# Four-layer convolution network on one core: one of every four hidden-layer evictions of the last stage moved from ScalarE to VectorE

## The chip, the cores and the metric

The kernel runs on one core of a Trainium2 chip, in one launch. Its time is the device time of that core in microseconds (us). Several executions are timed, and the median counts; one further execution is recorded by the hardware profiler, and all durations below come from that one.

## What is computed

The input is a batch of 1024 images of 16 x 16 positions with 16 channels, in float32. Four layers follow each other, each of the form x + layer(group norm of x). Layer 0 is a tensor-train product, layer 2 a 3 x 3 convolution, and layers 1 and 3 are one step of a cellular automaton. Layer 3 is the one that the change touches:

```python
def update(x):
    xt = jnp.transpose(x, (0, 3, 2, 1))
    B, _, W, Hh = xt.shape
    pre = _alive(xt)                       # 3x3 maximum of channel 3 > 0.1
    y1 = _depthwise(xt, conv1_w, conv1_b)
    y2 = _depthwise(xt, conv2_w, conv2_b)
    p = jnp.concatenate([xt, y1, y2], axis=1)
    flat = p.reshape(B * W * Hh, 48)
    h = jax.nn.relu(flat @ fc0_w.T + fc0_b)          # 128 hidden values
    d = (h @ fc1_w.T + fc1_b).reshape(B, C, W, Hh)
    xn = xt + d
    mask = (pre & _alive(d)).astype(xn.dtype)
    return jnp.transpose(xn * mask, (0, 3, 2, 1))
...
x = x + _L3_conv_ref(_gn(x), ...)
```

The reshape to 48 columns is taken as it stands: a "pixel" of the hidden layer is three neighbouring rows of the flattened array, so a hidden row r (there are 256) depends on rows 3r, 3r+1 and 3r+2 of the channels and their two depthwise results.

## The kernel before, in words

The batch is worked on in two chunks of 512 images, one image per column of a tile of 128 x 512. The stages follow each other on TensorE without a break; normalization, loads and stores of neighbouring chunks are woven in. The last stage is layer 3 on the second chunk (`layer_nca(X1, 1, 3, L3, xo)`, L1729). It alone is called with `xo`, the buffer in which the result is turned for the output. It takes 2735.4 to 3003 us of the profiled span.

**Quads.** The 256 hidden rows are grouped in fours, the quads (q, w2, v, hf): q counts four groups of channels, w2 eight pairs of columns, v the two of a pair. Quad m holds the rows j = 0 to 3 of `rows_of` (L1343); "row m.j" below is row j of quad m. Quads 0 to 15 are q = 0, 16 to 31 q = 1, and so on. In this stage the last four quads are cut in halves of 256 images (hf = 0 or 1), so there are 68 quads, of which 0 to 59 have full width (hf is None).

**Hidden rows (fc0, L1562).** A row needs two or three matmuls (L1562, `ph`), each of 32 input rows, so four rows run side by side in four row groups of the array (32 input rows each). In q = 0 most rows have two, later three. The row is summed in a PSUM bank of pool `h`, six banks. After the last matmul it is evicted: relu of the sum plus bias, into a `hid` tile (128 x 512, pool of eight). This is L1565, on ScalarE (`A.activation`).

**Second matrix (fc1, L1398).** For each quad four matmuls side by side read its four `hid` tiles into a bank of pool `o` (two banks), which is shared by the two quads v = 0 and v = 1 of one column pair. After v = 1, `finish` (L1404) reads the bank on VectorE: in q = 0 the alive flags of the result (L1406), always the sum with the layer's input (L1410).

**Masks (q = 0 only).** For each column pair the flags of the input (L1428, VectorE) and of the result are counted over neighbours by small matmuls (`pcnt`, L1437) into two banks of pool `h`, and VectorE makes the mask from the two counts (L1442, L1443). Then GpSimd applies it and adds the residual (L1449, L1450); in q > 0 it does so directly after L1410.

**Turning.** Each finished tile is transposed on TensorE (`ptx`, L1460, into a bank of pool `o`), and VectorE copies it out in two halves (L159; in this stage the helper `evac` uses VectorE alone). Beside that, `output_steps` turns the first chunk: for each of 16 image lines SP loads a tile, VectorE transposes it in four instructions (L1041), and SP stores it (L1046).

**Order.** Every engine works through its own queue in the order in which the program issues the instructions (`manual_schedule`). For this stage the order comes from `plan()` (L1489). It yields one step at a time: either the fc1 of a quad, or a list of at most four tiles, one for each row group. It knows the six banks and a model of the evictions: an eviction begins at the earliest 1.15 steps after the row's last tile, evictions follow each other at 0.75 steps, and a bank is free at the end of its eviction. Rows up to two quads ahead of the next fc1 may begin:

```python
evacs = max(evacs, t + (1.15 if quads[m][3] is None else 1.9))
evacs += 0.75 if quads[m][3] is None else 1.0
free_at.append(evacs)
```

The plan orders TensorE's matmuls, and with them the evictions: `tile_of_row` (L1539) issues an eviction directly after the last matmul of its row. Calls put off with `after(n, ...)` are issued n steps later, after that step's own work: the mask three steps after an fc1, the turning eight steps after the residual. `run` (L1575) issues the steps of `output_steps` at fixed shares of the stage's 262 steps: the transposes of line n after a share of 0.068 + 0.054 n.

Two rules of the pools are needed to follow the prediction. A bank or tile that is freed goes to the back of its pool's line, and the next use takes the one at the front; which use frees or takes first is a matter of program order. If all eight `hid` tiles are still held in program order, the eviction takes the one that was taken longest ago, and waits for the fc1 that reads it, though TensorE comes to that fc1 only later.

Of the kernel before, what the change touches and what calls it, by code (L numbers as in the profile page):

```python
# [11 lines left out]
AF = mybir.ActivationFunctionType  # L12
ALU = mybir.AluOpType
# [46 lines left out]
def row_tiles(r):  # L60

    lines = defaultdict(list)
    for s in range(3):
        ch, w = divmod(3 * r + s, S)
        if ch < C:
            lines[ch, w].append(s)
        else:
            for kw in range(3):
                if 0 <= w + kw - 1 < S:
                    lines[ch, w + kw - 1].append((s, kw))  # L70
    tiles = defaultdict(lambda: [None, None])
    for (ch, w), terms in lines.items():
        what = terms[0] if ch < C else TERMS.index(tuple(sorted(terms)))
        tiles[ch, w // 2][w % 2] = what
    return [(ch, pair, tuple(v)) for (ch, pair), v in sorted(tiles.items())]
# [13 lines left out]
def triple(wo):  # L89

    k, w = divmod(3 * wo, S)
    if w >= S - 2:
        n = 2 if w == S - 1 else 3
        return n, 12 + 3 * n
    return w % 2, 6 * k + 3 * (w % 2)
# [8 lines left out]
def conv_preact_kernel(ctx: ExitStack, tc: tile.TileContext, a: dict, out: bass.AP):  # L104
    nc = tc.nc
    V, A, G, T = nc.vector, nc.scalar, nc.gpsimd, nc.tensor
# [29 lines left out]
    def work(shape, tag, name, dt=F32):  # L136
        p, sizes = pool["sb"]
        return p.tile(shape, dt, tag=tag, name=name, bufs=sizes[tag])
# [3 lines left out]
    def bank(shape, tag, name):  # L142
        p, sizes = pool["ps"]
        if tag == "mw":
            either[0] ^= 1
            tag = "mw"[either[0]]
        return p.tile(shape, F32, tag=tag, name=name, bufs=sizes[tag])
# [61 lines left out]
    for d, v in ((0, 1), (2, 0)):  # L209
# [7 lines left out]
    nca = dict(  # L217
        xw=pack[:, 0:512].rearrange("p (n k) -> p n k", n=4),
        b1=pack[:, 512:513],
        bt=pack[:, 513:769],  # L220
        w1=pack[:, 769:833].rearrange("p (v m) -> p v m", v=2),
    )
# [1102 lines left out]
    def layer_nca(X, n, l, L, xo=None):  # L1325
# [9 lines left out]
        def cols(hf):  # L1335
            return slice(0, NB) if hf is None else slice(hf * NB // 2, (hf + 1) * NB // 2)

        def width(hf):
            return slice(0, NB if hf is None else NB // 2)
# [3 lines left out]
        def rows_of(q, w2, v):  # L1343
            return [16 * (4 * q + j) + 2 * w2 + v for j in range(4)]

        def weights(m):

            if m >= len(quads):
                return
            q, w2, v, hf = quads[m]  # L1350
            slot = triple(2 * w2 + v)[1]
            if hf == 1:
                st["wq", m] = st["wq", m - 4]
            elif q > 0:
                st["wq", m] = work([P, 3, HID], "wq", "wq")
                nc.sync.dma_start(
                    st["wq", m],
                    L["wy"][q - 1].rearrange("g v h s k -> (g v h) s k")[:, slot : slot + 3],
                )

        def lines(m):


            if m >= len(quads) or triple(2 * quads[m][1] + quads[m][2])[0] < 2:
                return
            nx = st["nx", m] = work([P, 2, NB], "nx", "nx")
            for r in rows_of(*quads[m][:3]):
                tiles = row_tiles(r)
                g = tiles[0][0] % 4
                over = [t[0] % C for t in tiles if t[0] % 4 != g]  # L1370
                c, n1 = over[0], len(over)
                nc.sync.dma_start(
                    nx[32 * g : 32 * g + 32, 0:n1],
                    X[32 * (c % 4) : 32 * (c % 4) + 32, 8 * (c // 4) : 8 * (c // 4) + n1],
                )
# [50 lines left out]
        def flags(w2):  # L1426
            f = st["f", w2] = work([P, NB], "f", "flags", BF16)
            V.tensor_scalar(f[96:128], X[96:128, w2], ALIVE, None, ALU.is_gt)  # L1428
# [92 lines left out]
        def step(slot):  # L1521
            def go():
                t = st["slot"]
                if isinstance(slot, int):
                    q, w2, v, hf = quads[slot]
                    fc1(q, w2, v, hf, [st["hid", slot, j] for j in range(4)])
                else:
                    for x in slot:
                        tile_of_row(*x)
                go.dense = isinstance(slot, int)  # L1530
                due = [fn for n, fn in later if n <= t]
                later[:] = [x for x in later if x[0] > t]
                for fn in due:
                    fn()
                st["slot"] = t + 1

            return go

        def tile_of_row(m, j, k):  # L1539
            q, w2, v, hf = quads[m]  # L1540
            r = rows_of(q, w2, v)[j]
            tiles = row_tiles(r)
            if k == 0:
                if st.setdefault("begun", -1) < m:
                    st["begun"] = m
                    weights(m + AHEAD)
                    lines(m + FAR)
                    if v == 0 and q == 0:
                        flags(w2)
                st["ph", m, j] = bank([P, NB], "h", "ph")[:, width(hf)]  # L1550
            ph = st["ph", m, j]
            ch, pair, pat = tiles[k]
            g = tiles[0][0] % 4
            rg = slice(32 * g, 32 * g + 32)
            if ch < C:
                w = nca["xw"][rg, XPATS.index(pat)]
            else:
                w = st["wq", m][rg, TRIPLES[triple(2 * w2 + v)[0]].index(pat)]

            x = X[rg, 8 * (ch % C // 4) + pair] if ch % 4 == g else st["nx", m][rg, pair]  # L1560
            x = x[:, cols(hf)]
            T.matmul(ph, w, x, start=k == 0, stop=k == len(tiles) - 1)  # L1562
            if k == len(tiles) - 1:
                h = st["hid", m, j] = work([P, NB], "hid", "hid")[:, width(hf)]
                A.activation(h, ph, AF.Relu, bias=nca["bt"][:, r : r + 1])  # L1565

        def rest():
            while later:
# [156 lines left out]
    with ExitStack() as es:  # L1725
        stage(es, dict(nca_sb, xs=2, xo=2), nca_ps)

        xo = X0.rearrange("p n b -> p (n b)").rearrange("p (g h w c) -> p g h w c", g=4, h=S, w=S)
# [29 lines left out]
```

## Time and profile before

| what | us |
|---|---|
| median of 3 runs | 3019.41 |
| lowest and highest run | 3018.77, 3025.02 |
| profiled execution | 3020.7 |
| its span, first to last instruction | 3018.9 |
| mean granted TensorE clock, share of full speed | 0.991 |
| last stage, in the span | 2735.4 to 3003 |
| TensorE busy there | 264.4 of 267.6 |
| ScalarE busy there | 166.9 |
| VectorE busy there | 118.0 |
| 240 full-width evictions on ScalarE there, L1565 | 153.5, 0.686 each |
| 32 half-width evictions there | 13.5, 0.472 each |

The page of a profile gives for each engine its busy time, the share of the span and the number of instructions; below that the span in 40 equal slices, where a digit is the busy share of a slice in tenths; then the chain of work that ended last, followed back from the last instruction. A group line has the source line, engine, operation, output and inputs, shapes and count, then the busy time in us and the mean of one in ns, then the idle time just ahead of these instructions with what ended it. A line of the timeline has the start in us, the duration in us, and in square brackets the idle time before it with its releaser. PE is TensorE's matmul, PEld its weight load, DVE VectorE, ACT ScalarE, POOL GpSimd. In the table by stretch the columns are the stretch, its length, and the busy time of PE, PEld, DVE, ACT and POOL with the number of instructions, then the granted clock, the share of DMA and GB/s. Ends of matmuls are modelled, so a TensorE that is shown busy can still be waiting; starts are not modelled. A float32 matmul has two records.

### The profile page before, as it was taken

The numbers are of one execution on the slowest core, as the hardware profiler recorded it, in microseconds if no ns is written. First come the engines' busy times: TensorE is split into PE (matmuls) and PEld (weight loads), VectorE is DVE, ScalarE is ACT, GpSimd is POOL, SyncE is SP. The second block draws the span as 40 slices with busy tenths as digits, with TensorE's granted clock in tenths as the row PEclk, the third lists the DMA queues.
The fourth block names the chain that finished last, engine by engine and source line by source line (L and its number), as shares of the span: only waits on it lengthen the run. The fifth ranks groups of instructions, "written<-read, shape, count | busy, mean of one in ns | idle before, by whom it ended". The sixth has DMA issues, their size and how long they took to land.

```text
span 3018.9 us, 36939 instructions
## 1 busy us (share of the span) xinstructions
PE 2968.3 (98%) x13876; PEld 1247.0 (41%) x13876; DVE 1765.1 (58%) x2352; ACT 1102.6 (37%) x1822; POOL 669.5 (22%) x727
## 2 busy tenths in 40 slices
PE   7999999999999999999999999999999999999997
PEld 5544334444444444444444433333333333333333
DVE  5354337555554555544555768856878766856433
ACT  4431441000000000000111146666667666666564
POOL 2035670200000000000000005434542323442321
PEclk8999999999999999999999999999999999999998
DMA  8643664533334433332222234445446866443466
GB/s 317 232 127 94 152 150 146 167 110 110 110 110 138 138 110 110 110 103 89 89 89 94 72 124 161 129 133 194 131 131 177 196 100 211 129 129 110 135 173 215
DMA packets 251523, 418.40 MB, mean 139 GB/s; under 512 B 34869, under 2 KB 105065, under 8 KB 248273
## 3 DMA queue, kind: packets, MB, share of 16 engines
q1 hardware_dynamic: 225776, 362.53, 36.6%
q0 software_dynamic: 25376, 53.38, 8.6%
q8 instruction: 110, 1.80, 0.3%
q14 instruction: 69, 0.56, 0.1%
q10 hardware_dynamic: 192, 0.13, 0.0%
HBM read 238.58 MB, written 165.53 MB: 134 GB/s over the span
## 4 chain that ended last, share of the span: by engine, by line
PE 90%; issue 2%; DVE 2%; DMA 2%; POOL 1%; ACT 1%; SPq 0%; POOLq 0%; DVEq 0%; ACTq 0%
PE po L1172 51%; PE ph L1562 21%; PE po L1398 8%; PE po L1260 3%; PE pw L1095 3%; PE L_conv_pe L392 1%; PE ptin L902 1%; PE po L1269 1%; DMA xn<-xf 1%; PE ptx L1460 1%; POOL res L1450 1%; POOL u L1449 1%; DVE sq L622 1%; PE pr L801 0%; DMA xn<-in_x_dram 0%
## 5 line engine op out<-in xcount | busy, mean ns | idle before, releaser
L1172 PE MATMUL po<-xn,w 128*128 128x512 f32 x3584 | 1577.4, 597 | 0.8 <-DVE xn L982 0.8
L1172 PEld LDWEIGHTS po<-xn,w 128*128 128x128 f32 x3584 | 671.7, 190 | 839.5 <-issue 820.9
L1565 ACT ACTIVATE hid<-ph,pack 128x512 f32<-128x512 f32 (+1 forms) x1040 | 655.6, 680 | 375.1 <-PE ph L1562 263.7
L1208 DVE TENSOR_TENSOR r<-r,po 128x512 f32<-128x512 f32 x576 | 378.2, 684 | 577.1 <-PE po L1172 524.7
L1449 POOL TENSOR_TENSOR u<-u,mask 128x512 f32<-128x512 f32 x123 | 193.8, 1576 | 1809.1 <-DVE mask L1443 1410.9
L1100 ACT COPY w<-pw 128x512 f32<-128x512 f32 (+1 forms) x320 | 150.6, 557 | 1209.6 <-issue 1006.4
L1562 PE MATMUL ph<-xn,wq 32*128 32x512 f32 (+1 forms) x3752 | 565.2, 599 | 0.0
L1562 PEld LDWEIGHTS ph<-xn,wq 32*128 32x128 f32 x3752 | 240.7, 184 | 263.9 <-issue 231.8
L1562 PE MATMUL ph<-xn,pack 32*128 32x512 f32 x1288 | 299.2, 625 | 4.6 <-DVE mask L1442 3.2
L1398 PE MATMUL po<-hid,pack 128*32 128x512 f32 (+1 forms) x2080 | 279.4, 600 | 0.0
L1113 DVE TENSOR_TENSOR w<-w 128x512 f32<-128x512 f32 x320 | 211.3, 687 | 86.6 <-ACT w L1100 86.6
L655 DVE TENSOR_TENSOR xn<-xn,m 128x1024 f32<-128x1024 f32 x160 | 216.3, 1383 | 35.5 <-ACT m L678 35.3
L1450 POOL TENSOR_TENSOR res<-res,u 128x512 f32<-128x512 f32 x123 | 204.5, 1663 | 9.6
L1410 DVE SCALAR_TENSOR_TENSOR u<-po,pack,xn 128x512 f32<-128x512 f32 (+1 forms) x130 | 96.3, 741 | 179.2 <-PE po L1398 175.1
L1260 PE MATMUL po<-xn,convw 128*128 128x512 f32 x368 | 163.9, 598 | 2.7 <-ACT conv L1310 2.7
L1562 PEld LDWEIGHTS ph<-xn,pack 32*128 32x128 f32 x1288 | 115.6, 186 | 105.2 <-issue 67.4
L1208 DVE TENSOR_TENSOR xn<-xn,po 128x512 f32<-128x512 f32 x96 | 64.4, 685 | 123.7 <-PE po L1172 123.3
L1398 PEld LDWEIGHTS po<-hid,pack 128*32 128x32 f32 x2080 | 42.8, 108 | 192.2 <-issue 134.3
L622 DVE TENSOR_TENSOR sq<-sq 128x1024 f32<-128x1024 f32 x75 | 106.2, 1416 | 11.1 <-ACT sq L640 10.4
L1260 PEld LDWEIGHTS po<-xn,convw 128*128 128x128 f32 x368 | 68.2, 190 | 97.8 <-issue 88.1
L404 POOL DMA_DIRECT2D L_conv_wy<-xn x160 | 88.8, 563 | 28.3 <-ACT xn L398 17.0
L1095 PE MATMUL pw<-R,gq 32*128 32x256 f32 (+1 forms) x1280 | 89.1, 384 | 1.0 <-DMA gq<-g_dram 1.0
(174 smaller groups left out, 1776.7 us busy)
## 6 DMA issues: line engine op xcount, KB each, us to landing
xf<-r SPq DMA_DIRECT2D x112, 512.0 KB, 3.8
xn<-xf SPq DMA_DIRECT2D x96, 512.0 KB, 4.7
r<-xf SPq DMA_DIRECT2D x80, 512.0 KB, 4.5
wq<-L_conv_wy SPq DMA_DIRECT2D x192, 192.0 KB, 2.7
res<-xf SPq DMA_DIRECT2D x128, 256.0 KB, 3.0
xf<-res SPq DMA_DIRECT2D x96, 256.0 KB, 2.0
res<-xr SPq DMA_DIRECT2D x256, 64.0 KB, 2.8
xf<-conv POOLq DMA_DIRECT2D x64, 256.0 KB, 5.9
```

The costliest lines, as they stand in the source:

```text
L655: V.tensor_tensor(part, part, m().unsqueeze(1).broadcast_to([P, 2, NB]), op)
L1095: T.matmul(pw[r][:, v], st["g", u][rows, v], st["R"][rows, p % 2, 64 * k0 : 256], start=True, stop=True,)
L1100: A.copy(w[:, k0:4, :, 32 * r : 32 * r + 32].rearrange("p k t (v o) -> p v (k t) o", v=2), pw[r],)
L1113: V.tensor_tensor(w[:, k], w[:, x], w[:, y], ALU.add if sign > 0 else ALU.subtract)
L1172: T.matmul(po, st["w", u][:, matrix, t], x, start=t == 0, stop=t == 3)
L1208: V.tensor_tensor(r[at], r[at], po, ALU.add if sign > 0 else ALU.subtract)
L1260: T.matmul(st["po", h][wh], conv["fw"][:, y], X[:, 16 * wh + h + y - 1], start=y == max(0, 1 - h), stop=y == min(2, S - h),)
L1398: T.matmul(po[32 * j : 32 * j + 32], nca["w1"][:, v], hid[j], start=v == 0, stop=v == 1)
L1449: by.tensor_tensor(u, u, st["m"][:, w2, cols(hf)], ALU.mult)
L1450: by.tensor_tensor(r, r, u, ALU.add)
L1562: T.matmul(ph, w, x, start=k == 0, stop=k == len(tiles) - 1)
L1565: A.activation(h, ph, AF.Relu, bias=nca["bt"][:, r : r + 1])
```

## The change

In the last stage, the eviction of row j = 3 of every full-width quad is issued as a `tensor_scalar` on VectorE (add the bias column, then the maximum with 0) in place of the `activation` on ScalarE. Rows 0 to 2, the half-width quads, and layer 1 and the first chunk of layer 3 stay as they were. The plan and its model of the evictions are not touched, nor is the order of TensorE's instructions.

```diff
@@ -1562,7 +1562,11 @@
             T.matmul(ph, w, x, start=k == 0, stop=k == len(tiles) - 1)
             if k == len(tiles) - 1:
                 h = st["hid", m, j] = work([P, NB], "hid", "hid")[:, width(hf)]
-                A.activation(h, ph, AF.Relu, bias=nca["bt"][:, r : r + 1])
+                if xo is not None and j == 3 and hf is None:
+
+                    V.tensor_scalar(h, ph, nca["bt"][:, r : r + 1], 0.0, ALU.add, ALU.max)
+                else:
+                    A.activation(h, ph, AF.Relu, bias=nca["bt"][:, r : r + 1])
```

## The prediction

> **What bounds the kernel now.** I read the page first: busy shares, slices, chain. TensorE is busy in every slice and is 90% of the chain of work that ended last.
>
> ```profile
> PE 2968.3 (98%) x13876; PEld 1247.0 (41%) x13876; DVE 1765.1 (58%) x2352; ACT 1102.6 (37%) x1822; POOL 669.5 (22%) x727
> ...
> PE   7999999999999999999999999999999999999997
> ...
> DVE  5354337555554555544555768856878766856433
> ACT  4431441000000000000111146666667666666564
> ...
> PE 90%; issue 2%; DVE 2%; DMA 2%; POOL 1%; ACT 1%; SPq 0%; POOLq 0%; DVEq 0%; ACTq 0%
> ```
>
> The change lies in the last stage, 2735.4 to 3003 us. Busy time by stretch there (q = 0; the irregular hand-over in q = 1; the regular rest) shows TensorE full, ScalarE at 56 to 69%, VectorE at 37 to 58%:
>
> ```profile
> 2735.40:2797.90 62.50, 62.50 (x460) 24.59 (x460) 36.33 (x59) 43.09 (x68) 13.57 (x12) 1.00 0.45 121
> 2797.90:2870.50 72.60, 70.99 (x527) 26.79 (x526) 29.54 (x51) 40.66 (x64) 22.87 (x19) 1.00 0.51 140
> 2870.50:2976.00 105.50, 105.50 (x870) 40.48 (x866) 38.69 (x70) 67.53 (x105) 31.67 (x26) 1.00 0.64 173
> ```
>
> "Busy" hides waits, so I laid the matmul records of L1562 and L1398 (1956, just what `plan()` orders) against its steps. A full step (one tile in each of four row groups, two records per matmul) takes 0.86 to 0.97 us, an fc1 0.99, a transpose group 0.58. In the regular rest every step has that length: TensorE waits for no eviction there, and a faster one gains nothing. In q = 0 the step after the mask counts is late in every pair of quads: its second and third rows start just as a ScalarE eviction ends (2771.24 then 2771.29; 2771.82 then 2771.82), because they reuse those banks.
>
> The groups by shape in this stage give the durations:
>
> ```profile
> L1041 DVE STREAM_TRANSPOSE xo<-xs 128x256 f32<-128x256 f32 x64 | 36.5, 652 | 0.0
> L159 DVE COPY xn<-ptx 128x256 f32<-128x256 f32 x60 | 31.5, 603 | 41.6 <-PE ptx L1460 41.6
> L1410 DVE SCALAR_TENSOR_TENSOR u<-po,pack,xn 128x512 f32<-128x512 f32 x31 | 23.3, 751 | 80.6 <-PE po L1398 79.7 <-POOL res L1450 0.4
> L1406 DVE TENSOR_SCALAR flags<-po,pack 32x512 bf16<-32x512 f32 x8 | 6.1, 758 | 12.7 <-PE po L1398 12.5
> ...
> L1442 DVE TENSOR_SCALAR mask<-pcnt 128x512 bf16<-128x512 f32 x8 | 5.5, 690 | 6.6 <-PE pcnt L1437 6.5
> ```
>
> The timeline of VectorE around one pair of q = 0 shows its queue nearly without gaps:
>
> ```profile
> 2767.76 0.76 DVE L1406 TENSOR_SCALAR flags<-po,pack 32x512 bf16<-32x512 f32 x1
> 2768.55 0.75 DVE L1410 SCALAR_TENSOR_TENSOR u<-po,pack,xn 128x512 f32<-128x512 f32 x1
> 2769.31 0.42 DVE L1428 TENSOR_SCALAR flags<-xn 32x512 bf16<-32x512 f32 x1
> 2769.75 2.31 DVE L1041 STREAM_TRANSPOSE xo<-xs 128x256 f32<-128x256 f32 x4
> 2771.92 0.69 DVE L1442 TENSOR_SCALAR mask<-pcnt 128x512 bf16<-128x512 f32 x1
> 2772.72 0.69 DVE L1443 SCALAR_TENSOR_TENSOR mask<-pcnt,mask 128x512 bf16<-128x512 f32 x1
> ```
>
> [...] L1406 at 2793.37 ran right behind four transposes, though its fc1 ended near 2791.1. [...] a tensor_scalar takes 423 ns from SBUF (L1428), 690 from PSUM (L1442). [...] L1410 keeps 751 ns with evictions running beside it.
>
> **What is removed and added.** 60 of the 272 evictions of this stage (quads 0 to 59, row 3; the half-width quads stay) leave ScalarE: 60 x 0.686 = 41 us of an engine that sets no end: no gain by itself. VectorE gets 60 tensor_scalar of 128x512 from PSUM with a bias column. The trace has none; the nearest are L1442 (0.69, constants) and L1406 (0.76, bias column and two operations, 32 partitions). I take 0.76; ends 0.69 and 0.80. 60 x 0.76 = 46 us come on top of the 118 us that VectorE is busy in these 267.6 us: it has room on average. No DMA is added, and the order of TensorE's work stays as `plan()` wrote it.
>
> What counts is the wait. An eviction waits for its last matmul and for the fc1 that frees its hid buffer: with 8 buffers for three quads under way that is often an fc1 that TensorE has yet to reach. On ScalarE only other evictions queue behind it. On VectorE these do: L1406 and L1410 (they free the fc1 bank), L159 (the transpose bank), the transposes, L1442 and L1443 (the count banks, reused by the next hidden rows). The 16 groups of transposes (2.3 us each) now run ahead into idle VectorE time; behind a waiting eviction they no longer can. `run()` hands out group n after a share of 0.068 + 0.054 n of the 262 steps: group 8 after step 130, so behind the eviction of row 37.3 in that step, though it ran 4.4 us before that step ended. In q = 0 a pair of quads (7.83 us) gives VectorE 0.76 + 0.75 + 0.42 + 0.69 + 0.69 + 1.06 = 4.4 us; two evictions make 5.9, a transpose group 8.2, more than the pair.
>
> Place by place, with times of the trace before (a delay is counted from there, so places add), each engine in its order, 0.05 us from an eviction's end to the matmul that waited for it (2771.24 to 2771.29 above):
> - Start: row 0.3's bank is wanted at 2739.01. VectorE finishes L655 at 2738.94, flags at 2739.38, then evicts to 2740.15 (ScalarE did by 2738.96); the matmul starts at 2740.2 rather than 2739.01, and ScalarE's lighter queue gives 0.1 of it back at most: **+1.1**.
> - 2752 to 2758: row 5.3 waits for fc1 to 2752.54, evicts to 2753.36; L1406, L1410, transposes, flags follow; L1442 ends 2758.3 instead of 2757.61, and its bank is wanted at 2757.77: **+0.6**.
> - 2763: row 7.3 is out at 2763.5, not 2763.99; the bank wait of 0.5 goes: **-0.5**.
> - 2767 to 2774 (shown above): row 8.3 waits for fc1 to 2767.61 and evicts to 2768.45; L159 to 2769.5, L1406 to 2770.3, L1410 to 2771.05, flags to 2771.5, row 9.3 to 2772.25, transposes to 2774.5, L1442 to 2775.1 instead of 2772.61. Its bank was taken for row 11.3 at 2772.83: **+2.3**.
> - 2775 to 2780: row 10.3 in the same way; row 11.3 is out near 2780.1; a count matmul of 2778.31 needs that bank, and with its three matmuls (0.65) it ends at 2780.8 in a row group that a hidden row took at 2779.70: **+1.1**.
> - 2791 to 2795: transposes hold VectorE to 2793.34, L1406 and L1410 to 2794.9; rows 15.3 and 16.3 to 2796.45. The latter's bank was taken at 2794.80, and the next row's at 2795.38: **+1.1**.
> - Row 29.3, behind transposes: **+0.1**. The other rows of q = 1 have over 1 us between eviction and use, and cost nothing.
> - 2882 to 2890: row 36.3 blocks to 2882.6, row 37.3 to 2886.4; the transposes that ran at 2879.93 now follow to 2889.4, L1410 to 2890.15; fc1 of quad 36 wanted that bank at 2889.65: **+0.5**.
> - 2929 to 2934: row 46.3 waits for L159 (2929.04), is out at 2929.8, fc1 wanted it at 2929.56: **+0.3**. Row 48.3 waits for that fc1 to 2931.0 and is out at 2931.75; transposes follow to 2934.05, row 47.3 to 2934.8; its fc1 was due at 2933.64: **+1.2**.
> - 2947: row 51.3 first, so L1410 and L159 end at 2945.5, transposes 2947.7, row 52.3 2948.45; bank wanted at 2948.19: **+0.3**. 2959: row 55.3, transposes (before at 2952.82), L1410 to 2962.95, fc1 due 2962.54: **+0.45**.
>
> Sum: 1.1 + 0.6 - 0.5 + 2.3 + 1.1 + 1.1 + 0.1 + 0.5 + 0.3 + 1.2 + 0.3 + 0.45 = 8.55, so **+8.5 us**. TensorE is full between the places, so nothing is caught up there. At 0.69 for the eviction some 18 of them on the path give 1.3 less, at 0.80 0.8 more.
>
> What is hidden: GpSimd starts later by what L1410 loses, at worst 2.9 us; 2890.15 + 2.5 = 2892.7 still precedes the transpose of 2894.43. SP's stores wait for transposes, but are issued late (2896.63 for those of 2879.93), 7 us after the new end; without that cover they would hold the weight loads.
>
> The profiled execution took 3020.7 us, span 3018.9 and 1.8 around it: 3029.2 expected of it. The median of the runs shown is 3019.41, 1.3 below that execution: **3027.9**.
>
> **Rivals.** (A) Absorbed: the delays of q = 0 (5.7 of the sum) fall into the waits that TensorE has in each pair there anyway, and half of the rest is caught up: +1.4, 3020.8. For it: most of the 60 rows have over 0.5 us between eviction and use. Against: the banks of the counts, and fc1, have almost none. (B) Not slower: two engines evict at once. The bank waits after the counts go: a count matmul of 2770.91 leaves its row group 0.22 later, the hidden row there began at 2771.88, so some 0.75 in each of six pairs: -4.5, 3014.9. It decides if VectorE reaches row 3 before ScalarE would have. For: rows 7.3, 9.3 and 16.3 are among the twelve waited for. Against: the other nine are rows 0 to 2, held by fc1, and 9.3 and 16.3 come later on VectorE. (C) VectorE becomes the bound wherever a transpose group lies: 16 groups at 1 us, the size of the larger places above: +16, 3035.4. Against: by the walk above only seven of them do harm. That the change does nothing is excluded: its condition holds for 60 rows.
>
> **Chances.** Forecast 0.75, A 0.14, B 0.04, C 0.07. A measurement here tells about 0.2%, 6 us, from no change. Slower: 0.70 of the forecast's, and C: 0.77. Within: 0.05 of it, A, half of B: 0.21. Faster: 0.02. Range: 3022.5 (a short eviction, and the places of 2.3, 1.2 and 0.6 absorbed: +3.1) to 3031.5 (a long one, and two more groups in the way at 1.4: +12.1). It leaves out C, B and half of A, 0.18.
>
> **What would show it.** Right: hid evictions on VectorE near 0.76 us; L1041 no longer ahead of its step; steps lengthened at 2739, 2774, 2780, 2795, 2890, 2934, and the regular quads between unchanged. Waits of TensorE that end with VectorE grow, those that end with ScalarE shrink. Wrong: these steps unchanged, VectorE finishing row 3 before ScalarE finishes its neighbours, or a VectorE eviction well off 0.76 us.

## The result, and the profile after the change

| what | before | after |
|---|---|---|
| median of 6 runs each, us | 3019.09 | 3031.32 |
| lowest and highest | 3018.02, 3025.02 | 3028.00, 3033.26 |
| profiled execution; its span | 3020.7; 3018.9 | 3032.55; 3030.8 |
| last stage, first matmul of step 0 to the start of the last matmul | 265.19 | 273.76 |
| part of the span ahead of the stage | 2735.38 | 2738.66 |

The ratio of the run times is 1.0032, 95% interval 1.0022 to 1.0042: 9.7 us slower, 6.6 to 12.7. The two medians of the table lie 12.2 us apart, near the upper end of that; a later comparison of the same two kernels (e12 below, 11 and 12 runs) has 1.0028. The forecast was 3027.9 (3022.5 to 3031.5), so the median of 3031.32 lies just inside its upper end. In the profiled executions the stage is 8.57 us longer; the forecast's sum was 8.55. The profiled execution itself was forecast at 3029.2 and took 3032.55: the remaining 3.3 us lie ahead of the stage, where no instruction differs, and the section on the clock says what they are.

The page of the changed kernel, its busy shares, the slices of VectorE and ScalarE, and the chain that ended last:

```profile
PE 2976.2 (98%) x13876; PEld 1247.4 (41%) x13876; DVE 1806.4 (60%) x2412; ACT 1069.1 (35%) x1762; POOL 669.4 (22%) x727
...
DVE  5355337555554555544555768756977766857554
ACT  4431441000000000000101156666667666664444
...
PE 90%; DVE 3%; DMA 2%; issue 2%; ACT 1%; POOL 1%; SPq 0%; DVEq 0%; ACTq 0%; POOLq 0%
```

Sixty instructions went from ScalarE to VectorE (2352 to 2412, 1822 to 1762), VectorE gained 41 us, and the chain is still TensorE's by 90%. Nothing on this page says why the kernel is slower; VectorE's share of the chain went from 2 to 3%.

The table by stretch of the changed kernel, with the same steps as in the prediction (columns as there):

```profile
2738.66:2807.80 69.14, 66.23 (x461) 25.15 (x461) 48.37 (x76) 33.74 (x51) 13.25 (x11) 0.98 0.40 109
2807.80:2880.60 72.80, 71.11 (x527) 26.88 (x526) 40.96 (x67) 31.34 (x48) 23.15 (x20) 1.00 0.50 139
2880.60:2987.70 107.10, 106.49 (x870) 40.33 (x866) 57.02 (x96) 53.25 (x79) 31.65 (x26) 1.00 0.62 170
```

The stretch of q = 0 grew from 62.50 to 69.14, the second hardly at all, the third from 105.50 to 107.10. In the first, TensorE now shows 2.9 us of idle time where it had none, and the granted clock is 0.98 instead of 1.00. VectorE is busy 70% of it, not 100%: it is not short of time on average.

The groups of VectorE by shape in the stage:

```profile
L1567 DVE TENSOR_SCALAR hid<-ph,pack 128x512 f32<-128x512 f32 x60 | 44.8, 749 | 76.2 <-PE po L1398 54.1 <-PE ph L1562 22.0
L1041 DVE STREAM_TRANSPOSE xo<-xs 128x256 f32<-128x256 f32 x64 | 36.3, 647 | 0.0
L159 DVE COPY xn<-ptx 128x256 f32<-128x256 f32 x60 | 31.6, 606 | 12.7 <-PE ptx L1460 12.7
L1410 DVE SCALAR_TENSOR_TENSOR u<-po,pack,xn 128x512 f32<-128x512 f32 x31 | 23.2, 747 | 15.5 <-PE po L1398 15.0
L1406 DVE TENSOR_SCALAR flags<-po,pack 32x512 bf16<-32x512 f32 x8 | 6.1, 758 | 0.6 <-PE po L1398 0.3
```

An eviction on VectorE takes 0.749 us, and its neighbours keep their durations to within 0.005 us of those before (L1041 0.647 for 0.652, L159 0.606 for 0.603, L1410 0.747 for 0.751, L1406 0.758 for 0.758). The telling columns are those of the idle time. Before the change L1410 had 80.6 us of idle time ahead of it, L159 41.6 and L1406 12.7: VectorE stood waiting for exactly these. Now it stands ahead of L1567 for 76.2 us, 54.1 of it for fc1 (L1398), which frees a hid tile, and the others follow with 15.5, 12.7 and 0.6. They have become late work.

VectorE's timeline for the pair of quads that the prediction showed (row 8.3, row 9.3, then the next pair's row 10.3), and below it the matmul of TensorE that waits:

```profile
2772.53 0.75 DVE L1567 TENSOR_SCALAR hid<-ph,pack 128x512 f32<-128x512 f32 x1 [2.36 <-PE po L1398]
2773.20 1.03 DVE L159 COPY xn<-ptx 128x256 f32<-128x256 f32 x2
2774.26 0.76 DVE L1406 TENSOR_SCALAR flags<-po,pack 32x512 bf16<-32x512 f32 x1
2775.05 0.75 DVE L1410 SCALAR_TENSOR_TENSOR u<-po,pack,xn 128x512 f32<-128x512 f32 x1
2775.82 0.42 DVE L1428 TENSOR_SCALAR flags<-xn 32x512 bf16<-32x512 f32 x1
2776.27 0.75 DVE L1567 TENSOR_SCALAR hid<-ph,pack 128x512 f32<-128x512 f32 x1
2776.94 2.23 DVE L1041 STREAM_TRANSPOSE xo<-xs 128x256 f32<-128x256 f32 x4
2779.06 0.66 DVE L1442 TENSOR_SCALAR mask<-pcnt 128x512 bf16<-128x512 f32 x1
2779.83 0.69 DVE L1443 SCALAR_TENSOR_TENSOR mask<-pcnt,mask 128x512 bf16<-128x512 f32 x1
2783.63 0.75 DVE L1567 TENSOR_SCALAR hid<-ph,pack 128x512 f32<-128x512 f32 x1 [3.10 <-PE po L1398]
...
2779.78 1.12 PE L1562 MATMUL ph<-xn,pack 32*128 32x512 f32 x2 [0.72 <-DVE mask L1442]
```

VectorE waits 2.36 us for an fc1, then works for 8.0 us with hardly a gap, and L1442, the one that TensorE needs, comes in the eighth row. A hidden row of TensorE starts only when L1442 is done, after 0.72 us in which all of TensorE stood still. After its work VectorE idles again for 3.10 us.

What TensorE itself waited for in this stage, by the records of its waits (the two rows of L1460 and the row of L1443 are in the kernel before with the same numbers; it had no others):

```profile
PE ptx L1460 <- DVE res L1450: 1.6, 1, 1.6
PE pcnt L1437 <- DVE hid L1567: 1.3, 2, 0.8
PE ptx L1460 <- DVE xn L159: 1.2, 1, 1.2
PE ph L1562 <- DVE hid L1567: 0.9, 1, 0.9
PE ph L1562 <- DVE mask L1442: 0.7, 1, 0.7
PE po L1398 <- DVE u L1410: 0.6, 2, 0.3
PE ph L1562 <- DVE mask L1443: 0.2, 1, 0.2
```

The new ones add to 3.5 us: two count matmuls and a hidden row that wait for a VectorE eviction, a hidden row behind L1442, two fc1 behind L1410. They are the engines and lines that the prediction named. The view shows only waits in which all of TensorE stood still; a wait of one row group beside three working ones is in the starts of the steps alone.

### The profile page after: what moved, and what is told of

The parts are those of the page before. It is cut to its first block, busy times and chain, and to the rows that moved or that the text cites. A ratio compares the mean times of both kernels' runs of the same rounds, so it can differ in the third digit from the quotient of the medians.

```text
span 3030.8 us, 37042 instructions
## 1 busy us (share of the span) xinstructions
PE 2976.2 (98%) x13876; PEld 1247.4 (41%) x13876; DVE 1806.4 (60%) x2412; ACT 1069.1 (35%) x1762; POOL 669.4 (22%) x727
## 4 chain that ended last, share of the span: by engine, by line
PE 90%; DVE 3%; DMA 2%; issue 2%; ACT 1%; POOL 1%; SPq 0%; DVEq 0%; ACTq 0%; POOLq 0%
PE po L1172 51%; PE ph L1562 21%; PE po L1398 8%; PE po L1260 3%; PE pw L1095 3%; PE L_conv_pe L392 1%; PE ptin L902 1%; PE po L1269 1%; PE ptx L1460 1%; DVE sq L622 1%; DMA xn<-xf 1%; DVE xn L655 1%; PE pr L801 0%; DMA xn<-in_x_dram 0%; POOL res L1450 0%
## 5 line engine op out<-in xcount | busy, mean ns | idle before, releaser
L1569 ACT ACTIVATE hid<-ph,pack 128x512 f32<-128x512 f32 (+1 forms) x980 | 622.1, 680 | 415.8 <-PE ph L1562 294.6
L1398 PE MATMUL po<-hid,pack 128*32 128x512 f32 (+1 forms) x2080 | 281.2, 602 | 0.7 <-DVE u L1410 0.6
L1410 DVE SCALAR_TENSOR_TENSOR u<-po,pack,xn 128x512 f32<-128x512 f32 (+1 forms) x130 | 96.1, 739 | 114.6 <-PE po L1398 110.9
L1398 PEld LDWEIGHTS po<-hid,pack 128*32 128x32 f32 x2080 | 43.2, 108 | 193.5 <-issue 129.6
L1567 DVE TENSOR_SCALAR hid<-ph,pack 128x512 f32<-128x512 f32 x60 | 44.8, 749 | 76.2 <-PE po L1398 54.1
```

The source lines that it names most:

```text
L1398: T.matmul(po[32 * j : 32 * j + 32], nca["w1"][:, v], hid[j], start=v == 0, stop=v == 1)
```

## The experiments

Each profiled run is compared by the starts of the plan's steps, which are the same in all of them. "Stage" is the distance from the first matmul of step 0 to the start of the last matmul; before it is 265.19 us. It comes from one profiled execution of each run; the two traces of the changed kernel differ by 0.28. The edits are shown against the changed kernel, those of e4, e5, e7 and e8 against the kernel before; `...` stands for lines left out.

| run | stage, us | against before | ratio of run times, 95% interval |
|---|---|---|---|
| changed kernel | 273.76 | +8.57 | 1.0032 (1.0022 to 1.0042) |
| e1, quads 0 to 15 only | 271.25 | +6.06 | 1.0024 (1.0016 to 1.0032) |
| e2, quads 16 to 59 only | 267.68 | +2.49 | 1.0013 (1.0006 to 1.0020) |
| e3, changed, no transposes | 267.37 | +2.18 | 1.0008 (1.0000 to 1.0016) |
| e4, before, no transposes | 265.62 | +0.43 | 1.0001 (0.9993 to 1.0009) |
| e5, before, 10 hid tiles | 261.72 | -3.47 | 0.9983 (0.9976 to 0.9990) |
| e6, changed, 10 hid tiles | 266.26 | +1.07 | 1.0006 (0.9999 to 1.0013) |
| e7, added work without a wait | 266.86 | +1.67 | 1.0005 (0.9997 to 1.0014) |
| e8, both engines, one after the other | 277.33 | +12.14 | 1.0050 (1.0035 to 1.0065) |
| e9, the wait with a third of the work | 267.03 | +1.84 | 1.0013 (1.0006 to 1.0020) |
| e10, eviction in two halves | 279.76 | +14.57 | 1.0046 (1.0029 to 1.0063) |
| e11, 10 hid tiles, three rows on VectorE | 260.90 | -4.29 | 0.9986 (0.9977 to 0.9994) |
| e12, changed kernel again | 273.48 | +8.29 | 1.0028 (1.0018 to 1.0038) |

The theory on trial: the cost sits at a few places, where VectorE's queue stands behind an eviction that waits. The rivals: VectorE's added busy time or a contest for PSUM, spread over all evictions; the wait alone, whatever is queued behind it; absorbed.

### e1 and e2: where the cost is

```diff
-                if xo is not None and j == 3 and hf is None:
+                if xo is not None and j == 3 and q == 0:              # e1
+                if xo is not None and j == 3 and hf is None and q > 0:  # e2
```

> VectorE evicts row 3 of the 16 quads of q = 0 only. Queue theory (the cost lies at the places where VectorE's queue stands behind an eviction): the places of q = 0 in the prediction add to +5.7, so the stage from its first to its last matmul grows by 5.0 to 6.6 us, and nothing changes after 2810 us. The changed kernel had one stretch of 3.4 us at half clock in q = 0, at 2781; without it its stage would be some 1.7 us shorter, and q = 0 of this run shows whether that stretch belongs to the pause before it or to chance. Rival, cost in proportion to the evictions moved (0.14 us each, as from a slower eviction or a contest for PSUM): 16 of 60, so +2.3. Rival, absorbed: +0.5 or less.

> VectorE evicts row 3 of quads 16 to 59 only. Queue theory: the places there add to +2.85 (0.1 for row 29.3, then 0.5, 0.3, 1.2, 0.3, 0.45); the changed kernel had +1.9 there; so +1.7 to +3.0 for the stage, all of it in a handful of steps, and with the run on quads 0 to 15 the sum of the changed kernel (8.6, or about 7 without the stretch at half clock). Rival, in proportion: 44 of 60, so +6.3, spread over all steps. Rival, absorbed: below 0.5.

Measured: +6.06 and +2.49, together 8.55 against 8.57 for the whole. Sixteen of the 60 evictions bring 71% of the cost, so a cost in proportion is excluded (it asked for +2.3 and +6.3). In e1 the steps from 52 to the end move by 0.13 in all; in e2 the largest increments are at steps 135 (+0.42) and 179 (+0.79), the same as in the changed kernel (+0.42, +0.78).

### e3 and e4: without the transposes behind the eviction

```diff
         def turn(h, st):
-            st["o"] = work([P, 4, S, S], "xo", "xo")
-            x = st["x"].rearrange("p w (j f) -> p f w j", f=4)
-            for f in range(4):
-                V.transpose(
-                    st["o"][:, f].rearrange("p (w v) c -> p w c v", v=2), x[:, f]
-                )
+            st["o"] = st["x"]
...
-                st["o"].rearrange("p f w c -> p f (w c)"),
+                st["o"].rearrange("p (f w) j -> p f (w j)", f=4),
```

> The changed kernel without VectorE's 64 transposes of the first chunk's output; that half of the output is stored as it was loaded, unturned. Queue theory: with 36 us less on VectorE, and no group of 2.3 us behind a waiting eviction, most places fall away (2767, 2791, 2882, 2929, 2959; what stays is the start, 1.1, and about 0.6 at 2752): +1.0 to +2.8 against the kernel before without transposes. Rival, the wait of VectorE for fc1 alone makes the cost, whatever else VectorE has to do: +7 or more. Rival, contest for PSUM: unchanged, +8.

> The kernel before without the 64 transposes of the first chunk's output; that half of the output is stored unturned. It is the yardstick for the changed kernel without them. Both theories: the transposes lie beside other work in the kernel before, so the stage keeps its length within 0.5 us.

Measured: 267.37 against 265.62, +1.75. So 6.8 of the 8.57 us are there only because 16 groups of transposes share VectorE's queue with the evictions, though in the kernel before the same transposes cost nothing (e4: +0.43). (Some 0.6 of the 6.8 is a stretch at half clock, which the changed kernel has in this stage and e3 has not; see e12.) What stays is the start (+1.20), a count matmul behind an eviction (+0.73, steps 39 and 40) and smaller terms of both signs. The evictions and their waits are all still there (66.5 us of idle time for fc1 ahead of them, against 54.1 in the changed kernel), so the wait alone, and a contest for PSUM, are excluded as the main cause.

### e5 and e6: without the wait for fc1

```diff
-        stage(es, dict(nca_sb, xs=2, xo=2), nca_ps)
+        stage(es, dict(nca_sb, xs=2, xo=2, hid=10, wq=4), nca_ps)
```

> The kernel before with 10 instead of 8 hid tiles in the last stage (and 4 instead of 5 tiles for the weights wq, to make room). With 10 an eviction of ScalarE hardly ever waits for an fc1 that TensorE has yet to reach. Queue theory: in q = 0 the rows that TensorE starts just as an eviction ends (2763, 2771, 2779, 2786 in the trace before, some 0.5 to 0.7 each) then find their bank free: the stage 2.0 to 3.5 us shorter, all of it before 2800. Rival, those waits come from ScalarE's own rate and not from the hid tiles: within 0.5 of before.

> The changed kernel with 10 hid tiles (and 4 tiles for wq). VectorE does the same work, in the same order, but its evictions wait for an fc1 far less often. Queue theory: the places where L1406, L1410, L1442 and the transposes stand behind a waiting eviction go, the start (+1.2) and the few waits at row 46.3 stay: the stage +0.5 to +2.5 us against the kernel before, so 6 to 8 below the changed kernel. Rival, VectorE's added 45 us are what costs, wait or no wait: +7 or more.

That the wait did go is seen in the idle time ahead of the evictions in the stage. ScalarE's full-width group in the kernel before:

```profile
L1565 ACT ACTIVATE hid<-ph,pack 128x512 f32<-128x512 f32 x240 | 153.5, 686 | 91.1 <-PE ph L1562 65.7 <-PE po L1398 24.1
```

The same group with 10 tiles (e5), where 24.1 us for fc1 have become 1.4:

```profile
L1565 ACT ACTIVATE hid<-ph,pack 128x512 f32<-128x512 f32 x240 | 150.8, 688 | 92.3 <-PE ph L1562 89.1 <-PE po L1398 1.4
```

VectorE's evictions with 10 tiles (e6), where the 54.1 us of the changed kernel have become 3.6:

```profile
L1567 DVE TENSOR_SCALAR hid<-ph,pack 128x512 f32<-128x512 f32 x60 | 44.9, 749 | 62.3 <-PE ph L1562 58.1 <-PE po L1398 3.6
```

Measured: the kernel before gains 3.47 us in the stage. Only 1.73 of that lies in q = 0, where all of it was expected; 0.81 comes at step 87, where fc1 of quad 24 waited for evictions that were held by fc1 of quad 23 (ScalarE's timeline before has 2.76 us of idle time for L1398 ahead of 2837.50), and 0.6 in the half-width quads. The changed kernel falls from +8.57 to +1.07, as expected. But the fair yardstick is the kernel with 10 tiles: against that the move of the evictions still costs 266.26 - 261.72 = 4.54. So the wait for fc1 accounts for 4.0 of the 8.57, not for nearly all as the expectation had it. The rest is plain queueing: L1442 still comes behind a group of transposes (+1.07 at step 35), a count matmul behind two evictions that follow transposes (+1.42 at step 51), the start stays (+1.15), and L159 is late once (+0.89 at step 87).

### e7, e8 and e9: work and wait apart

```diff
+            if xo is not None:
+                st["own"] = pool["sb"][0].tile([P, 564], F32, tag="own", name="own", bufs=1)
+                G.memset(st["own"], 1.0)
...
                 A.activation(h, ph, AF.Relu, bias=nca["bt"][:, r : r + 1])
+                if xo is not None and j == 3 and hf is None:
+                    V.tensor_tensor(st["own"], st["own"], st["own"], ALU.max)
```

> The kernel before (ScalarE evicts every row), and VectorE does 60 tensor_tensor operations of 128x564 on a tile of its own in SBUF, about 0.75 us each, issued where the changed kernel issues its evictions. The added work is not part of the computation; it waits for nobody and nobody waits for it. Queue theory: +0.5 to +2.5 us for the stage (the transposes and L1406 pushed back by 0.75 here and there). Rival, busy time alone makes the cost: +7 or more.

Measured: +1.67. The work was more than in the changed kernel, 58.7 us, because the mean below is a mixture: 35 of the 60 operations took 0.70 to 0.75 us, as intended, among them all 16 of q = 0; the other 25 took 0.92 to 1.71, and every one of these ran beside a `tensor_tensor` of GpSimd. VectorE's group of the added operations:

```profile
L1570 DVE TENSOR_TENSOR own<-own 128x564 f32<-128x564 f32 x60 | 58.7, 978 | 0.8
```

So VectorE's time, without a wait, is nearly free here.

```diff
-                A.activation(h, ph, AF.Relu, bias=nca["bt"][:, r : r + 1])
+                if xo is not None and j == 3 and hf is None:
+                    A.activation(h[:, 32:NB], ph[:, 32:NB], AF.Relu, bias=nca["bt"][:, r : r + 1])
+                    V.tensor_scalar(
+                        h[:, 0:32], ph[:, 0:32], nca["bt"][:, r : r + 1], 0.0, ALU.add, ALU.max
+                    )
+                else:
+                    A.activation(h, ph, AF.Relu, bias=nca["bt"][:, r : r + 1])
```

> Row 3 of each full-width quad evicted by both engines: ScalarE columns 32 to 511, VectorE columns 0 to 31. VectorE has the same 60 waits for the last matmul and for fc1 as in the changed kernel, and hardly any work [...]. Queue theory: the waits alone hold back what is queued behind them, but only until fc1; without the 0.75 us of each eviction VectorE catches up: +0.7 to +2.5 us. Rival, the wait alone makes the cost: +6 or more. If both this and the run with the work alone are small, the cost of the changed kernel is in their product: a queue that is held until late and then has more to do than fits before the banks are wanted.

Measured: +12.14, far from the expectation. The experiment did not do what it was meant to. VectorE's part, which reads the same bank and writes the same hid tile, waits for ScalarE's, as its group shows:

```profile
L1567 DVE TENSOR_SCALAR hid<-ph,pack 128x32 f32<-128x32 f32 x60 | 14.9, 250 | 115.1 <-ACT hid L1566 114.9
```

So VectorE's queue was held longer than in the changed kernel: until fc1, then through ScalarE's queue, then through 0.66 us of eviction. With a third of the busy time that the changed kernel adds (14.9 against 44.8) and a longer wait, it costs more than the changed kernel does, so VectorE's busy time cannot be what costs here. But the row itself is also finished later, as its two parts follow each other, and how much of the 12.14 that makes was not separated. e9 has the wait of the changed kernel without that addition:

```diff
+                x = hid[j]
+                if xo is not None and j == 3 and hf is None:
+                    x = x[:, None, 0:32].to_broadcast([P, 16, 32])
...
-                    po[32 * j : 32 * j + 32], nca["w1"][:, v], hid[j], start=v == 0, stop=v == 1
+                    po[32 * j : 32 * j + 32], nca["w1"][:, v], x, start=v == 0, stop=v == 1
...
-                    V.tensor_scalar(h, ph, nca["bt"][:, r : r + 1], 0.0, ALU.add, ALU.max)
+                    V.tensor_scalar(
+                        h[:, 0:32], ph[:, 0:32], nca["bt"][:, r : r + 1], 0.0, ALU.add, ALU.max
+                    )
```

> The changed kernel, but VectorE's eviction of row 3 takes only the first 32 of 512 columns (some 0.25 us instead of 0.75), and ScalarE evicts nothing of that row; fc1 reads these 32 columns 16 times over, so TensorE does the same work, and the other 480 columns of row 3 are left out of the computation. Each eviction waits for what it waits for in the changed kernel, ahead of the same queue. Queue theory, by the same places: the ones at 2752, 2763, 2767 and 2791 lose 0.5 us for each eviction in them, the start goes to about +0.7: +0.8 to +2.5 us for the stage. Rival, the wait alone, whatever follows it: +6 or more.

The evictions of e9 on VectorE (its lines are three further down; L1401 is fc1):

```profile
L1570 DVE TENSOR_SCALAR hid<-ph,pack 128x32 f32<-128x32 f32 x60 | 14.9, 250 | 88.6 <-PE po L1401 63.5 <-PE ph L1565 24.8
```

Measured: +1.84. The idle time for fc1 is even longer (63.5 against 54.1 us), and yet the cost is small. Not every place shrank by 0.5 an eviction: step 35 still comes 1.77 late; but step 34 and the start gain 0.8 and 0.5 on the changed kernel, and from q = 1 on nothing is left. The work without the wait costs 1.67, the wait with a third of the work 1.84, both in full 8.57 (some 8.0 without the stretch at half clock, which neither e7 nor e9 has in this stage): the cost is in the combination, which is the case that e8's expectation had set out. By the run times e9 costs 3.9 us (1.8 to 6.0), more than its stage shows but still less than the changed kernel.

### e10: the duration of the eviction

```diff
-                    V.tensor_scalar(h, ph, nca["bt"][:, r : r + 1], 0.0, ALU.add, ALU.max)
+                    for b in (slice(0, NB // 2), slice(NB // 2, NB)):
+                        V.tensor_scalar(
+                            h[:, b], ph[:, b], nca["bt"][:, r : r + 1], 0.0, ALU.add, ALU.max
+                        )
```

> The changed kernel, VectorE's eviction of row 3 made of two instructions of 256 columns each; by the 256-column rows of VectorE (0.47 to 0.48) about 0.93 us in all, some 0.15 to 0.19 more than one of 512. Queue theory: the prediction had some 18 of the 60 evictions on the path, so 18 x 0.17 = 3 more than the changed kernel: +10.5 to +13.5 us against before. Rival, all 60 evictions cost in proportion: 60 x 0.17 = 10 more, +18 or over. Rival, only the waits count: +8.6 as in the changed kernel.

Measured: +14.57, but this number cannot be taken as it is. Just after the pause at the start, which is 1.1 us here, TensorE's clock was halved for 10 us (the number after the last bracket is the granted clock):

```profile
2741.55:2751.70 10.15, 10.15 (x42) 3.15 (x40) 1.82 (x5) 2.11 (x4) 0.00 (x0) 0.50 0.62 155
```

From the start of step 4 to that of step 10 the run lost 4.83 in that stretch, the changed kernel nothing. Without them it would be +9.7, 1.2 more than the changed kernel where 3 was expected. That comparison still leaves the changed kernel its own stretch at half clock, which e10 has not: with the 1.4 of its lengthened steps taken out too, the difference is 2.6. So it is 1.2 to 2.6; all 60 in proportion (10 more) is excluded. The run times do not show the profiled execution as an exception: all four of e10 (3034.69 to 3037.43) lie above every run of the changed kernel (3033.26 at most). Whether the clock falls at the start in each of them is not known. How many evictions lie on the path is not settled by this run.

### e11: rows chosen by place

```diff
-                if xo is not None and j == 3 and hf is None:
+                if xo is not None and (m, j) in ((7, 3), (11, 0), (13, 0)):
```

(with the pools of e5)

> The kernel before with 10 hid tiles and 4 tiles for wq, and of all rows only 7.3, 11.3's neighbours 11.0 and 13.0 evicted by VectorE: three rows for which, by the queues, VectorE would be through earlier than ScalarE, at banks that TensorE waits for. The run with 10 hid tiles alone had a stage 3.5 us shorter than before. Theory that a choice by place can gain: another 0.5 to 1.2, so -4.0 to -4.7. Rival, any eviction on VectorE only delays: -3.5 or less gain.

Measured: -4.29, so three evictions on VectorE shorten the stage of e5 by another 0.82, in the steps 28, 40 and 46, whose banks they free. By the run times e5 and e11 (0.9983 and 0.9986) cannot be told apart; both are faster than the kernel before and the changed one. The gain of these versions comes from the two additional hid tiles; the choice of engine adds little.

### e12 and the granted clock

> The changed kernel once more, for the stretch of 3.4 us at half clock that its first trace had at 2781 behind a pause of TensorE of 0.7. If the pause always brings it, it is there again and the stage is 8.5 to 8.7 us longer than before. If it depends on how the pause falls against the clock's own grid, it can be missing; then the stage shows what the waits alone cost: 7 to 8.4, the two steps at half clock (1.4 longer) back to their length and part of that waited for elsewhere.

The changed kernel's first trace has a stretch at half clock in q = 0, 1.4 us after TensorE had stood still for 0.72 us to wait for L1442; the second trace has it too. The table by stretch of the first trace, with the granted clock after the last bracket:

```profile
2779.50:2781.00 1.50, 1.22 (x4) 0.47 (x5) 0.91 (x2) 0.10 (x1) 0.40 (x1) 1.00 0.35 122
2781.20:2784.60 3.40, 3.40 (x19) 0.92 (x21) 0.97 (x2) 0.69 (x1) 1.82 (x2) 0.50 1.02 237
2784.70:2787.00 2.30, 2.30 (x21) 0.47 (x19) 2.24 (x5) 0.69 (x1) 0.00 (x0) 1.00 0.86 280
```

The second trace (e12), for the stretch at half clock alone:

```profile
2779.05:2782.40 3.35, 3.35 (x20) 1.21 (x16) 2.16 (x4) 0.69 (x1) 1.21 (x1) 0.50 0.98 227
```

e1 has the same pause and the same stretch (at 2781.3), and so has e8 (a pause of 0.73, a stretch at 2779.1). So in the three traces with the changed kernel's q = 0 the stretch followed the pause each time; the expected shorter stage without it was not seen. It does not always follow: pauses of 0.66 and 0.65 us for the same L1442 in e9 and e10 brought none, nor did the pause of 0.9 at the start of the stage in the changed kernel, e1, e3 and e12, nor one of 0.87 at 2782 in e3. The grid shows in the first trace: its stretch at 2781.20 starts 719 times 3.4133 us after the one at 327.02.

The 3.3 us ahead of the stage are in the main of the same kind. Where the code is the same, the first trace of the changed kernel has a clock of 0.79, 0.79 and 0.83 in the stretches 324 to 332, 395 to 403 and 2336 to 2346, the kernel before 1.00 in all three; at 1798 to 1810 it is the other way round, 0.86 against 0.72. In us at half clock that is 3.4 each, so (3 - 1) x 3.4 / 2 = 3.4. Laid against the kernel before matmul by matmul, this trace has two smaller terms besides, -0.6 in the first 90 us and +0.7 near 2399, which nearly cancel. The second trace of the changed kernel has 1.00 in the first two stretches, 0.83 in the third and 0.72 at 1798 to 1810, and its stage starts at 2735.79, 0.4 after that of before.

## Why the prediction was right

The mechanism, the sum and most of its terms held. By its own places, with the growth between the steps concerned in the first trace:

| place (times before) | forecast | measured |
|---|---|---|
| start, row 0.3 | +1.1 | +1.20 |
| 2752 to 2758, L1442 behind row 5.3 | +0.6 | +0.70 |
| 2763, bank wait gone | -0.5 | -0.39 |
| 2767 to 2774, rows 8.3, 9.3, transposes, L1442 | +2.3 | +2.40 |
| 2775 to 2780, row 11.3 and a count matmul | +1.1 | +1.80 |
| 2791 to 2795, rows 15.3, 16.3 | +1.1 | +0.90 |
| q = 1 | +0.1 | +0.29 |
| row 36.3, L1410, fc1 of quad 36 | +0.5 | +0.42 |
| row 46.3 | +0.3 | +0.16 |
| row 47.3 behind 48.3 and transposes | +1.2 | +0.63 |
| row 52.3 | +0.3 | 0 |
| row 55.3, L1410, fc1 54 | +0.45 | +0.33 |
| half-width quads | 0 | +0.13 |
| sum | +8.55 | +8.57 |

**What was removed** gained nothing, as said: ScalarE's 41 us less are nowhere in the step times. **The duration** of the new eviction was taken as 0.76 and is 0.749. **The moved transposes**: in the kernel before a group ran at 2879.93, ahead of its step:

```profile
2879.93 2.27 DVE L1041 STREAM_TRANSPOSE xo<-xs 128x256 f32<-128x256 f32 x4
2886.53 0.75 DVE L1410 SCALAR_TENSOR_TENSOR u<-po,pack,xn 128x512 f32<-128x512 f32 x1 [4.33 <-PE po L1398]
```

In the changed kernel it follows row 37.3, with L1410 behind it, as VectorE's timeline there shows:

```profile
2896.61 0.75 DVE L1567 TENSOR_SCALAR hid<-ph,pack 128x512 f32<-128x512 f32 x1 [3.03 <-PE po L1398]
2897.28 2.30 DVE L1041 STREAM_TRANSPOSE xo<-xs 128x256 f32<-128x256 f32 x4
2899.41 0.78 DVE L1410 SCALAR_TENSOR_TENSOR u<-po,pack,xn 128x512 f32<-128x512 f32 x1
```

The order eviction, transposes, L1410 is the one written down in advance, and fc1 of quad 36 (step 135) moved by 0.42. **Nothing caught up**: between the places the steps keep their lengths, so Rival A falls. **Rival B** needed VectorE to reach row 3 sooner than ScalarE; it does at 2763 (-0.39), and e11 shows that such rows exist, but there are few. **Rival C** asked for harm at each of the 16 groups of transposes; e3 shows that the transposes carry most of the cost, yet only at the places named. VectorE kept to the order of its queue, as the timeline at 2772 shows: L1442 ran at 2779.06, after the transposes (2776.94, for 2.23), although the last of its count matmuls began at 2775.8 and took 0.37.

One sign that the prediction named did not come: waits of TensorE that end with ScalarE were to shrink. Its matmuls have none in either trace, and those of its weight loads that end with ScalarE went from 9.7 to 10.2 us in the stage. Nor did ScalarE itself stand less behind fc1: the idle time for it ahead of the full-width evictions is 34.4 us with 180 of them, and was 24.1 with 240.

Four terms were off in size. The count matmul at 2775 to 2780 was 0.7 dearer: steps 35 and 36 ran at half clock for the most part, 1.4 longer, after the pause that the change itself had made. A change of clock was not among the prediction's steps. In e10, whose clock was full there, the place costs +1.18, near the forecast's 1.1, so some 0.6 of the 1.80 is the clock's, and the rest of the 1.4 lies beside a wait that would have been there anyway. In q = 1 the growth of 0.2 at one step, the fc1 of quad 24, was not foreseen; the forecast had put its 0.1 at row 29.3. The places of rows 47.3 and 52.3 were 0.9 too dear together. The walk added durations end to end, while in the timeline below the transposes start 0.09 before row 48.3 ends (2942.00 against 2942.09) and row 47.3 starts 0.10 before they end (2944.14 against 2944.24), and row 48.3 could start 0.4 earlier than put (2941.34 below, less the 10.76 by which this trace is late there, is 2930.58, not 2931.0). VectorE's timeline of the changed kernel, rows 48.3 and 47.3 around the transposes:

```profile
2941.34 0.75 DVE L1567 TENSOR_SCALAR hid<-ph,pack 128x512 f32<-128x512 f32 x1 [1.05 <-PE po L1398]
2942.00 2.24 DVE L1041 STREAM_TRANSPOSE xo<-xs 128x256 f32<-128x256 f32 x4
2944.14 0.71 DVE L1567 TENSOR_SCALAR hid<-ph,pack 128x512 f32<-128x512 f32 x1
```

From the start of row 48.3 to the end of row 47.3 that is 3.51, not 0.75 + 2.3 + 0.75 = 3.8. So the agreement of the sum to 0.02 is partly luck: +0.7 at the count matmul and +0.2 in q = 1 against -0.9 here. The claim that 0.04 more for an eviction costs 0.8 (some 18 evictions on the path) was not confirmed: e10 has 1.2 to 2.6 where it asked for 3, and is disturbed by the clock.

What the prediction put in one word, "the wait", the runs split in two: 4.0 us go when the wait for fc1 goes, 6.8 when the transposes go. They overlap, since at most places it takes both.

## What to carry to other kernels

Before moving work to an engine with idle time, write down the queue it enters: the price here was not the busy time (e7, 58.7 us for 1.67) but what stands behind an instruction that waits for a slower engine's next step, and what of that has a due time. Work that used to run ahead in the gaps, like the transposes here, is the first to be pushed in front of something urgent. Here, where evictions waited for a buffer, two more buffers (e5) were worth more than another engine.

## What the runs showed of the hardware that was not expected

TensorE's clock fell to half after some of its pauses, with 3.41 us to a stretch (at 2781.20 in the changed kernel) or a multiple of that (10.24 at 77.85 there). Within that trace the stretches start on one grid: at 327.02, 398.70 and 2781.20, of which the second is 71.68 us after the first, 21 times 3.4133, and the third 719 times. The pauses before its stretches were 0.26 us (ahead of 398.70) to 2.57 us long (ahead of 1804.99), and a pause was not followed by one each time (0.66 in e9, 0.65 in e10, 0.9 at the start of the stage). What decides it was not shown. By these figures the pause of 0.72 us could cost up to 1.7 us more (an estimate: half of 3.41; it came to some 0.6 at the place above), and the stretch of 10 us in e10, after a pause of 1.1, cost 4.83. Two executions of one kernel differ for this alone: in the windows above the two traces of the changed kernel have four stretches of 3.41 against three, 1.7 us.

The `tensor_scalar` from PSUM took 0.749, 0.479 and 0.250 us for 512, 256 and 32 columns (changed kernel, e10, e9): 0.22 us and 1.04 ns a column.

The `tensor_tensor` operations of VectorE that e7 added took 0.70 to 0.75 us where GpSimd ran none, and up to 1.71 beside one of GpSimd's (some beside one for part of their time stayed at 0.72 to 0.74). No run here isolates the reason.
